# Layer 0 of a hybrid convolution and attention kernel: x's first products on whole columns, the group sums later, and the copies of the last inverse placed around the exponential

## The chip, the cores and the metric

The kernel runs on one core of one Trainium2 chip. The metric is the device time of one execution in microseconds (us). Three executions of the kernel before gave 2968.66, 2972.97 and 2974.31 us, so the median is 2972.97 us. A profile was taken of a further execution, which took 2970.21 us.

## The reference, cut to what matters

The program is two layers on x of shape (4, 32, 128, 128): 4 batches, each of 32 images of 128 x 128 float32. Layer 0 is a neural operator with attention, layer 1 is an additive attention with a mixture of experts. Only layer 0 is touched here. Of it this matters:

```
x = x + L0(_gn(x))                      # _gn: 32 groups along the last axis
...
xn = _inorm(xa)                         # each image for itself
k = _fno_layer(xn, Kcw, Ksw, 64, 64)    # 32 heads: low modes times weights, and a skip
q = _fno_layer(xn, Qcw, Qsw, 64, 64)
v = _fno_layer(xn, Vcw, Vsw, 128, 128)
scores = einsum('bntk,bnsk->bnts', q, k) / 64
p_attn = softmax(scores)                # 32 x 32 for each head
av = einsum('bnts,bnsk->bntk', p_attn, v)
p = _fno_layer(av, Pcw, Psw, 128, 128)
a = _inorm(p + xa)
m = _fno_layer(_inorm(a), m0cw, m0sw, 128, 128, inner_norm=True, act=True)   # gelu
m = _fno_layer(m, m1cw, m1sw, 128, 128, inner_norm=True)
out = _inorm(m) + a
```

An `_fno_layer` is a real Fourier transform of an image, a product with complex weights on the low modes, and the inverse transform. All transforms are done here as matrix products with tables of cosines and sines.

## The kernel before, in words

Layer 0 is `layer0` (L131). It handles the four batches one after the other (the loop `for b in range(B)`, L895); layer 1 follows, from about 890 us on, with an order of its own that is written out by hand and isn't touched.

**Who sets the order.** In layer 0 a planner orders the instructions of each engine. It goes by program order as a priority, by its own estimate of the durations, and by buffers. Tiles come from pools; tiles of one tag share a ring of so many buffers (`bufs`), and a tile waits for its ring's next buffer. The helper `behind(later, earlier)` (L144) adds an order between two instructions without any data between them. PSUM has the tags "a", "b" and "wide", each a ring of two. SBUF has among others the tags "z" (2), "v" (3), "pr" (6) and "fold" (2).

**Opening.** x of batch 0 is loaded, `image_rows` and `image_moments` (L386, L410) sum each image and its square, `group_moments` and `image_scales` (L422, L438) turn that into the factor and offset of each group. `image_scales` also spreads factor and offset of the 32 groups over all partitions: the product `bg` with a matrix of ones, tag "a" (L448), copied to `by_group`, which is read only in the value stage (L925). `value_weights` (L600) and L813 to L834 prepare the weights of values, keys and queries on VectorE.

**Spectra of x**, `spectra_of_images` (L481), in four groups of 8 images. `half_rows` (L285) multiplies each image as the stationary operand with 66 of the 128 columns of the table `rows`: the products `pz`, tag "a", four images to a tile, which ScalarE copies to `z`. `columns_of` (L495) multiplies two images of `z` with 68 of the 101 columns of `colg`: the products `it`, tag "b", copied to `fold`. `unfold` (L509, products `em` and `std`) makes the modes `xe`, `xm` and `xx` of 16 images; `edge_row` (L562) makes a single further mode. `image_weights` (L465) makes the factor of each image from the sums `my`, tag "a", placed behind the first group.

**Attention weights**, `attention_weights` (L645). `xp` is a copy of `xe` in PSUM, `hm` a masked copy of `xx`. The products `so` (L669) and `sp` (L700, from products `pa` on VectorE and `pb` on GpSimd or VectorE) give the scores `sc` (L715 to L725), with `spt`, a copy of `sp`, in between (L705). VectorE takes maximum and difference, ScalarE the exponential `ex` (L732), VectorE sum and reciprocal, GpSimd the product `ph` (L742). `ph` goes to DRAM and comes back as `pr` (L758, L762).

**Value stage** (L945 to L998). For 5 slices of modes and 4 groups of images, `xb` is broadcast from DRAM, copied to PSUM as `xw`, multiplied with the table `gb` of value weights (products `u`: L972 on GpSimd, L976 on VectorE, tag "pr"), and summed on TensorE with `pr` as `po` (L909). Products of `turn` and `skip` (`pxt`, `sk`) come in between. The table `gb` is made once, in the opening, by `spread_values` (L623): 32 products `gw` in two passes each, tag "wide", each pair copied by ScalarE. `skip_matrix` (L767) makes `bd` from `ph` with the products `cm`, the VectorE products `cd` (tag "v") and the sums `cp`.

**Rest of a batch.** Inverse transform, spectra of layer m0 (L1156), gelu, then the spectra of layer m1 (L1248), with the products `pz` of `first_step` (L305, 128 columns, tag "a"). The last inverse brings m1's modes `spec` back: `negative` (L1066) puts a negated copy in front of the modes, `row_products` (L334) gives `y` for 16 images in two tiles of the tag "wide", ScalarE copies four images at a time to `v`, `inv` turns these to `four` (L359, tag "b"), and VectorE adds `four` to the batch's `xr`, each image with its own factor `c3` (L1344). ScalarE scales the gelu's images, `g` = `c2` x `g` + `cq`, in 32 instructions (L1296), GpSimd adds them to `xr` in four (L1306).

**Passage from one batch to the next.** While the m1 part of batch b is under way, the next batch's `image_scales` (L1246), `spectra_of_images` (L1288) and `attention_weights` (L1333) run too. Three hooks put batch b's scaling in between: 16 scalings behind `hm` and ahead of `spt`, 8 behind `spt` and ahead of the exponential, 8 behind the exponential. The last inverse of batch b follows (L1361). All products of the value stage of batch b + 1 are ordered behind the last `four` of that inverse (`mixed = [inverted]`, L905).

Of the kernel before, what the change touches and what calls it, by code (L numbers as in the profile page):

```python
# [13 lines left out]
P = 128  # L14
# [116 lines left out]
def layer0(  # L131
# [153 lines left out]
    def half_rows(images, z, last):  # L285

        for k in range(0, GI, 4):
            pz = ps.tile([P, 4, 2, KY], F32, name="pz", tag="a")
            for j in range(4):
                mm = nc.tensor.matmul(  # L290
                    pz[:, j],
                    images[k + j],
                    rows.rearrange("p (r x) -> p r x", r=2)[:, :, :KY],
                    start=True,
                    stop=True,
                )
# [37 lines left out]
    def row_products(spec, a, ahead=()):  # L334


        wide = [ps.tile([P, 2, 512], F32, name="y1", tag="wide") for _ in range(2)]
        for slot in range(4):
# [22 lines left out]
    def back(spec, a, take, ahead=(), copy=None, apart=False):  # L361

        wide = row_products(spec, a, ahead)
        for g in range(4):
            four, inverted, _ = four_images(
                wide,
                g,
                copy or evacuate,
                dict(tag="pr", bufs=6) if apart and a else dict(tag="v", bufs=3),
                "a" if apart and g % 2 else "b",  # L370
            )
            take([image(a, g, k) for k in range(4)], four)
# [65 lines left out]
    def image_scales(sv, gm, gv, shift):  # L438
# [5 lines left out]
        both = small.tile([P, 2, 32], F32, name="both", tag="both")  # L444
        nc.vector.tensor_scalar(both[:, 0], of_group, gr, None, ALU.mult)
        nc.vector.tensor_scalar(both[:, 1], of_group, gs, -1.0, ALU.mult, ALU.mult)
        by_group = small.tile([P, 2, 32], F32, name="by_group", tag="by_group")
        nc.vector.tensor_copy(by_group, sums("bg", ones, both, "a"))  # L448
# [14 lines left out]
        return by_group, colg, shift, sv, sv_op  # L463
# [17 lines left out]
    def spectra_of_images(b, xt, normed, then=None):  # L481


        _, colg, shift, sv, _ = normed
# [10 lines left out]
        def columns_of(g, z):  # L495
# [3 lines left out]
            it = ps.tile([P, GI // 2, 2 * n], F32, name="it", tag="b")  # L499
            for j in range(GI // 2):  # L500
                mm = nc.tensor.matmul(
                    it[:, j], z[:, 2 * j : 2 * j + 2].rearrange("p t r x -> p (t r x)"), colg[:, : 2 * n], start=True, stop=True
# [4 lines left out]
            nc.scalar.copy(folded[g // half][:, k : k + GI // 2], it)  # L507
# [74 lines left out]
        for g in GROUPS:  # L582
            z = grp.tile([P, GI, 2, 32], F32, name="z", tag="z")
            made = half_rows([xt[:, g + t] for t in range(GI)], z, z32[:, :, g : g + GI])
            if g == 0:
                ysc, scaled = image_weights(sv, made)
            if g == GI and then is not None:
# [10 lines left out]
        return xx, (xe, xm), xd, edges, ysc  # L598

    def value_weights():  # L600
# [8 lines left out]
        behind(nc.vector.tensor_scalar(p1, pw[:, :, :KA, 0], hv[:, 3:4], None, ALU.add), normed[4])  # L609
        of_row = []  # L610
        for ri, (b, d, op) in enumerate(
            ((v_re, v_im, ALU.subtract), (v_im, v_re, ALU.add))
        ):
            g = grp.tile([P, KX // 4, KY], F32, name=f"g{ri}", tag="v", bufs=3)
            behind(nc.vector.tensor_scalar(g, pw[:, :, :, ri], hv[:, 2:3], None, ALU.mult), normed[4])
# [7 lines left out]
    def spread_values(of_row):  # L623

        n = KX * KY // 8
        picked = grp.tile([P, 2, 4, 8, 16], F32, name="picked", tag="z")
        for k in range(2):
            nc.scalar.copy(picked[:, k], steps(ident[:, 64 * k :], [1, 4], [0, 8], [4, 16]))
        for q in range(4):
            for k in range(2):  # L630
                rows_of = picked[:, k, q].rearrange("p s n -> p (s n)")
                for ri in range(2):
                    to = ps.tile([P, 2, 512], F32, name="gw", tag="wide")[:, :, :n]
                    for h in range(2):
                        nc.tensor.matmul(
                            to[:, h], rows_of, of_row[ri][:, n * h : n * h + n], start=True, stop=True
                        )
                    nc.scalar.copy(
                        gb[:, k, ri, 2 * n * q : 2 * n * q + 2 * n].rearrange("p (h m) -> p h m", h=2), to
                    )  # L640
# [4 lines left out]
    def attention_weights(b, front, hooks=None):  # L645

        xx, (xe, xm), _, (x32, w32), _ = front
        xs = per_image("xs")
        nc.vector.tensor_copy(xs, xx[:, :, KY])
# [8 lines left out]
        nc.scalar.activation(hm[:, :, 1:], xx[:, :, 1:masked], AF.Identity, scale=high)  # L658
# [1350 lines left out]
```

## Time and profile before

| What | Value |
|---|---|
| Median of three executions | 2972.97 us |
| Profiled execution, whole | 2970.21 us |
| Profiled execution, span from first to last instruction | 2968.5 us |
| Busy: TensorE, VectorE, ScalarE, GpSimd | 2754.0, 2187.5, 2323.7, 2028.2 us |
| Granted TensorE clock, mean | 0.979 of full |
| Opening: first instruction to the first product `po` | 0 to 83.35 us |
| First passage: last gelu of batch 0 to the first `po` of batch 1 | 217 to 291 us |
| Time from one passage to the next | 205 us |

How to read it: "PE" is TensorE's products, "PEld" its weight loads, "DVE" VectorE, "ACT" ScalarE, "POOL" GpSimd, "SP" the queue that issues DMAs. L12 is line 12 of the kernel. A float32 product is two instructions in the trace. In a timeline a line gives start, duration, engine, line, operation, out<-in, shape and how many; in brackets is the idle time of the engine before it and what ended that. In the chain of waits a line gives start, duration and what.

### The profile page before, as it was taken

How to read it: one execution, taken by the hardware profiler on the slowest of the kernel's cores; microseconds unless marked ns; L12 is line 12 of the kernel's file. 1: busy time of each engine (PE TensorE's matmuls, PEld its weight loads, DVE VectorE, ACT ScalarE, POOL GpSimd, SP SyncE). 2: the span in 40 equal slices, each digit the busy share in tenths (PEclk: the TensorE clock that was granted, in tenths of full speed). 3: DMA queues.
4: the chain of work that ended last, by engine and by line, in shares of the span. 5: the costliest groups of instructions: out<-in, count | busy, mean ns of one | idle time of the engine just before them, and what ended most of it. 6: DMA issues, size and time to landing. Idle time of an engine off the chain costs nothing.

```text
span 2968.5 us, 52711 instructions
## 1 busy us (share of the span) xinstructions
PE 2754.0 (93%) x19506; PEld 1364.1 (46%) x19506; DVE 2187.5 (74%) x4934; ACT 2323.7 (78%) x3235; POOL 2028.2 (68%) x1801
## 2 busy tenths in 40 slices
PE   8888988988878999999899999989999999999997
PEld 5465564664644443344444343444444343444443
DVE  4876787778866677775678688667778766878877
ACT  3554555456359999899899999989999998999991
POOL 1703605417208987878987878898787889798773
PEclk8998999999989999999999999999999999999998
DMA  3403304205021101002010100111010020000000
GB/s 93 126 1 70 117 1 106 81 9 152 14 61 33 33 1 40 8 16 57 1 26 15 26 15 8 42 25 31 15 26 15 10 56 15 26 13 21 15 15 14
DMA packets 151154, 107.72 MB, mean 36 GB/s; under 512 B 36303, under 2 KB 140018, under 8 KB 150898
## 3 DMA queue, kind: packets, MB, share of 16 engines
q1 hardware_dynamic: 147633, 102.26, 13.3%
q8 instruction: 154, 2.52, 0.4%
q10 hardware_dynamic: 3264, 2.10, 0.3%
q14 instruction: 103, 0.84, 0.1%
HBM read 63.86 MB, written 19.50 MB: 28 GB/s over the span
## 4 chain that ended last, share of the span: by engine, by line
PE 60%; POOL 12%; ACT 11%; DVE 10%; issue 6%; DMA 0%; POOLq 0%; DVEq 0%; ACTq 0%
PE d L1799 20%; PE po L1818 11%; PE px L1705 6%; ACT r L1849 5%; PE n L1799 4%; POOL e L1858 3%; PE po L909 3%; POOL e L1857 3%; POOL u L972 2%; ACT e L1865 2%; DVE r L1854 2%; POOL kx L1464 2%; PE pz L305 2%; DVE xc L1709 1%; PE px L1106 1%
## 5 line engine op out<-in xcount | busy, mean ns | idle before, releaser
L1854 DVE TENSOR_TENSOR r<-n,r 128x1024 f32<-128x1024 f32 (+1 forms) x1056 | 961.5, 952 | 478.6 <-PE n L1799 391.1
L1857 POOL TENSOR_TENSOR e<-r 128x512 f32<-128x512 f32 x528 | 674.0, 1277 | 270.2 <-DVE r L1854 269.6
L1849 ACT ACTIVATE r<-d 128x1024 f32<-128x1024 f32 (+1 forms) x1056 | 793.4, 803 | 64.7 <-PE n L1799 56.8
L1861 ACT ACTIVATE r<-r 128x1536 f32<-128x1536 f32 x528 | 783.6, 1484 | 16.7
L1858 POOL TENSOR_TENSOR e<-e,r 128x512 f32<-128x512 f32 x528 | 671.6, 1272 | 41.4
L1799 PE MATMUL d<-qe,ke 32*128 32x512 f32 (+3 forms) x2304 | 606.4, 602 | 39.4 <-ACT r L1849 35.0
L1818 PE MATMUL po<-e,kx 128*128 128x512 f32 (+3 forms) x1152 | 594.8, 605 | 17.4 <-POOL e L1870 17.4
L1799 PE MATMUL n<-qe,ke 32*128 32x512 f32 (+3 forms) x2304 | 606.3, 602 | 0.0
L1799 PE MATMUL n<-qf,kf 32*128 32x512 f32 (+3 forms) x2304 | 553.1, 555 | 0.0
L1799 PE MATMUL d<-qf,kf 32*128 32x512 f32 (+3 forms) x2304 | 551.8, 555 | 0.0
L1709 DVE SCALAR_TENSOR_TENSOR xc<-px,wgt,xc 128x128 f32<-128x128 f32 x1024 | 358.0, 350 | 42.1 <-PE px L1705 10.6
L1865 ACT ACTIVATE e<-e 128x512 f32<-128x512 f32 x528 | 325.8, 617 | 66.6 <-POOL e L1858 65.7
L1818 PEld LDWEIGHTS po<-e,kx 128*128 128x128 f32 x1152 | 175.8, 188 | 395.2 <-issue 309.7
L1799 PEld LDWEIGHTS d<-qe,ke 32*128 32x128 f32 x2304 | 176.6, 183 | 358.8 <-ACT r L1849 339.1
L1799 PEld LDWEIGHTS d<-qf,kf 32*128 32x128 f32 x2304 | 220.5, 186 | 175.7 <-issue 163.4
L1705 PE MATMUL px<-we,x2t 128*128 128x512 f32 x512 | 265.7, 605 | 6.7 <-DVE xc L1709 5.5
L972 POOL TENSOR_TENSOR u<-xb,gb 128x858 f32<-128x858 f32 (+1 forms) x112 | 219.7, 1994 | 56.9 <-PE po L909 53.3
L1799 PEld LDWEIGHTS n<-qf,kf 32*128 32x128 f32 x2304 | 228.3, 185 | 19.5 <-issue 11.7
L1123 POOL TENSOR_TENSOR spec<-part,part 128x512 f32<-128x512 f32 x16 | 25.3, 1578 | 304.0 <-DVE part L1120 110.8
L976 DVE TENSOR_TENSOR u<-xw,gb 128x858 f32<-128x858 f32 (+1 forms) x208 | 214.8, 1101 | 5.1 <-PE po L909 2.9
L1799 PEld LDWEIGHTS n<-qe,ke 32*128 32x128 f32 x2304 | 177.6, 183 | 9.4 <-DVE r L1854 0.9
L909 PE MATMUL po<-u,pr 128*32 128x429 f32 (+1 forms) x1280 | 150.4, 525 | 27.3 <-POOL u L972 17.7
(421 smaller groups left out, 3398.5 us busy)
## 6 DMA issues: line engine op xcount, KB each, us to landing
xb<-xd SPq DMA_DIRECT2D x128, 214.5 KB
xc<-x SPq DMA_DIRECT2D x29, 512.0 KB
x<-x SPq DMA_DIRECT2D x16, 512.0 KB
qf<-qe SPq DMA_DIRECT2D x64, 128.0 KB
out<-xc SPq DMA_DIRECT2D x15, 512.0 KB
x<-in_x SPq DMA_DIRECT2D x14, 512.0 KB
xb<-xd SPq DMA_DIRECT2D x32, 198.0 KB
kf<-ke SPq DMA_DIRECT2D x32, 128.0 KB
```

What stands on the lines that cost most here:

```text
L909: mm = nc.tensor.matmul(*args, **kw)
L972: weighed = nc.gpsimd.tensor_tensor(u, xb, gk, ALU.mult)
L1705: nc.tensor.matmul(px, x2t[:, k * P : (k + 1) * P], we[:, e0 : e0 + 4], start=True, stop=True)
L1709: nc.vector.scalar_tensor_tensor(xc[:, k], px[:, e], wgt[:, k, e0 + e : e0 + e + 1], xc[:, k], ALU.mult, ALU.add)
L1799: nc.tensor.matmul(o, k, q, start=turn == 0 or g > 0, stop=turn == 1 or g > 0)
L1818: nc.tensor.matmul(sums[c, h][:, q0 : q0 + c1 - c0], kx[:, jb], e[:, c0:c1], start=jb == 0, stop=is_last and q0 > 2 * P, skip_group_check= ...
L1849: nc.scalar.activation(r[:, g], d, AF.Ln, scale=1.0 / DSCALE)
L1854: nc.vector.tensor_tensor(r[:, g], part, r[:, g], ALU.mult)
L1857: nc.gpsimd.tensor_tensor(e, r[:, 1], r[:, 2], ALU.add)
L1858: nc.gpsimd.tensor_tensor(e, e, r[:, 0], ALU.add)
L1861: nc.scalar.activation(r, r, AF.Exp, scale=-1.0)
L1865: nc.scalar.activation(e, e, AF.Exp)
```

## The change

All edits are in layer 0.

1. `half_rows` uses all 128 columns of `rows`, `columns_of` all 101 of `colg`; the copies that follow take the same part as before.
2. `bg` and `by_group` leave `image_scales`. The product stands behind the third group's `pz` in `spectra_of_images`, and ScalarE copies it. In the opening, `my` stands behind the second group, not the first.
3. Opening: key and query weights come ahead of `value_weights`. Three of the value weights' steps go from VectorE to ScalarE, behind the last copy of `fold`. All `gw` products are behind the last `sc`; 9 of the 16 copies stay on ScalarE, 7 go to VectorE, and all but the first two are behind the exponential or the reciprocal.
4. `xs` and `xh` are made by ScalarE.
5. Batches 0 to 2: GpSimd multiplies the modes `spec` by the factor (`c3s`, made of `c3` by two VectorE operations), behind the second row's products `pb`; VectorE adds `four` in one instruction of 512 elements. The adds of the first half are behind the reciprocal.
6. Batches 0 to 2: the scalings are placed 4 ahead of `hm`, 24 behind `xh` and ahead of `spt` (with `negative` after the 16th image), 4 behind `spt`. Half of the first `row_products` is behind the last product of `sp`, half behind the last of `sc`. The first copy `v` and its `four` stand ahead of the exponential, the others behind it. The copies `xw` are behind the last copy `v`.

```diff
-            pz = ps.tile([P, 4, 2, KY], F32, name="pz", tag="a")
+            pz = ps.tile([P, 4, 2, KX], F32, name="pz", tag="a")
...
-                    rows.rearrange("p (r x) -> p r x", r=2)[:, :, :KY],
+                    rows.rearrange("p (r x) -> p r x", r=2),
...
-    def row_products(spec, a, ahead=()):
-        wide = [ps.tile([P, 2, 512], F32, name="y1", tag="wide") for _ in range(2)]
-        for slot in range(4):
+    def row_products(spec, a, ahead=(), slots=range(4), wide=None):
+        wide = wide or [ps.tile([P, 2, 512], F32, name="y1", tag="wide") for _ in range(2)]
+        for slot in slots:
...
-    def back(spec, a, take, ahead=(), copy=None, apart=False):
-        wide = row_products(spec, a, ahead)
+    def back(spec, a, take, begun=(), copy=None, apart=False):
+        wide, *ready = begun or [row_products(spec, a)]
         for g in range(4):
-            four, inverted, _ = four_images(
...
+            four, inverted, roots["v"] = (
+                ready[g]
+                if g < len(ready)
+                else four_images(
...
-        both = small.tile([P, 2, 32], F32, name="both", tag="both")
-        nc.vector.tensor_scalar(both[:, 0], of_group, gr, None, ALU.mult)
-        nc.vector.tensor_scalar(both[:, 1], of_group, gs, -1.0, ALU.mult, ALU.mult)
-        by_group = small.tile([P, 2, 32], F32, name="by_group", tag="by_group")
-        nc.vector.tensor_copy(by_group, sums("bg", ones, both, "a"))
...
-                    it[:, j], z[:, 2 * j : 2 * j + 2].rearrange("p t r x -> p (t r x)"), colg[:, : 2 * n], start=True, stop=True
+                    it[:, j], z[:, 2 * j : 2 * j + 2].rearrange("p t r x -> p (t r x)"), colg, start=True, stop=True
...
-            if g == 0:
+            if g == (GI if b == 0 else 0):
                 ysc, scaled = image_weights(sv, made)
+            if g == 2 * GI:
+                groups = sums("bg", ones, both, "a")
+                behind(summing["bg"], made)
+                nc.scalar.copy(by_group, groups)
...
-        behind(nc.vector.tensor_scalar(p1, pw[:, :, :KA, 0], hv[:, 3:4], None, ALU.add), normed[4])
+        behind(nc.scalar.activation(p1, pw[:, :, :KA, 0], AF.Identity, bias=hv[:, 3:4]), roots["fold"])
...
-            g = grp.tile([P, KX // 4, KY], F32, name=f"g{ri}", tag="v", bufs=3)
-            behind(nc.vector.tensor_scalar(g, pw[:, :, :, ri], hv[:, 2:3], None, ALU.mult), normed[4])
+            g = grp.tile([P, KX // 4, KY], F32, name=f"g{ri}", tag="fold")
+            behind(nc.scalar.activation(g, pw[:, :, :, ri], AF.Identity, scale=hv[:, 2:3]), roots["fold"])
...
+                        behind(mm, scored)
...
+                    if ri and (q or k):
+                        behind(nc.vector.tensor_copy(part, to), inverted)
+                    else:
+                        copied = nc.scalar.copy(part, to)
+                        if q or k:
+                            behind(copied, softmax)
...
-        nc.scalar.activation(hm[:, :, 1:], xx[:, :, 1:masked], AF.Identity, scale=high)
-        copied = nc.scalar.activation(hm[:, :, 0], xx[:, :, 0], AF.Identity, scale=half_high)
+        ahead = hooks[4](copied) if hooks else None
+        copied = nc.scalar.activation(hm[:, :, 1:], xx[:, :, 1:masked], AF.Identity, scale=high)
+        if ahead is not None:
+            behind(copied, ahead)
+        nc.scalar.activation(hm[:, :, 0], xx[:, :, 0], AF.Identity, scale=half_high)
...
+        nc.scalar.copy(xs, xx[:, :, KY])
+        copied = nc.scalar.activation(xh, xx[:, :, KY], AF.Copy, scale=0.5)
...
+            if yy == 1 and hooks:
+                hooks[5](on_pool)
...
                     if x0 == 0:
-                        behind(c, weights[4])
+                        behind(c, roots["v"] if b else weights[4])
...
+            def first_ones(copied):
+                for t in range(ones_ahead):
+                    act = scale(t)
+                    behind(act, copied)
+                return act
+            def factored(on_pool):
+                product = nc.gpsimd.tensor_tensor(
+                    spec[:, :, 64:], spec[:, :, 64:], c3s.unsqueeze(2).to_broadcast([P, GI, P]), ALU.mult
+                )
+                behind(product, on_pool)
             def first_half(copied, on_pool):
-                for t in range(T // 2):
+                for t in range(ones_ahead, late_ones):
                     act = scale(t)
                     behind(act, copied)
+                    if t == 2 * GI - 1:
+                        behind(negative(spec, slice(0, GI)), act)
...
+            def third_quarter(scores, copied):
+                for t in range(late_ones, T):
+                    act = scale(t)
+                    behind(act, copied)
+                ready.append(act)
+                begun.append(row_products(spec, 0, (scores,), range(2)))
+                return add_scaled(images_of[2])
+            def begin(scored):
+                row_products(spec, 0, (scored,), range(2, 4), begun[0])
+                begun.append(four_images(begun[0], 0, nc.scalar.copy))
+                behind(begun[1][2], ready[0])
+                return begun[1][2]
...
-                for j, t in enumerate(images):
-                    nc.vector.scalar_tensor_tensor(
-                        xr[:, t], four[:, j], c3[:, t : t + 1], xr[:, t], ALU.mult, ALU.add
-                    )
+                g = images[0] - 16 * a
+                to = xr[:, 16 * a : 16 * a + 16].rearrange("p (k t) c -> p k t c", k=2)[:, :, g : g + 2]
+                added = nc.vector.tensor_tensor(to, to, four.rearrange("p (k t) c -> p k t c", k=2), ALU.add)
+                if a == 0:
+                    behind(added, weights[7])
```

## The prediction, made before the changed kernel was run

> **What bounds the kernel now.** I read the page's first part, then the busy times by stretch, then the chain of waits of the first 320 us, then each engine's timeline in the two places that the change touches. Tensor work fills 93% of the span, but layer 1 (from about 890 us) is not touched; only layer 0 can move, and there the chain runs through the opening (0 to 93 us) and, three times, through the passage from one batch to the next (217 to 292 us in the first). The stretches (us, then busy time with its count of TensorE, weight loads, VectorE, ScalarE, GpSimd, then granted clock, DMA share, GB/s):
>
> ```profile
> 22.00:46.00 24.00, 23.89 (x138) 22.53 (x138) 10.57 (x49) 8.18 (x28) 0.00 (x0) 0.51 0.00 1
> 221.00:225.00 4.00, 0.52 (x3) 0.43 (x3) 3.72 (x14) 0.01 (x1) 1.26 (x1) 0.76 0.00 0
> 225.00:235.00 10.00, 9.87 (x85) 7.55 (x84) 4.68 (x11) 1.98 (x4) 0.00 (x0) 0.76 0.01 2
> 278.00:293.00 15.00, 12.48 (x86) 5.06 (x84) 12.44 (x37) 4.08 (x8) 5.20 (x4) 0.90 0.39 105
> 293.00:355.00 62.00, 56.51 (x718) 30.55 (x720) 53.54 (x53) 37.32 (x83) 50.04 (x26) 1.00 0.52 158
> ```
>
> The opening's products of x run with TensorE full at half clock for 24 us. At 221 TensorE stands still. The value stage (293 to 355) is filled by three engines at once, so its length stays and its start decides.
>
> TensorE's timeline, opening and first passage:
>
> ```profile
> 18.77 0.38 PE L380 MATMUL mg<-tot,cst 128*128 128x2 f32 x2 [0.60 <-DVE tot L425]
> 21.79 0.66 PE L380 MATMUL bg<-both,ones 128*128 128x64 f32 x2 [2.64 <-DVE both L446]
> 220.70 0.38 PE L380 MATMUL d<-y,cst 128*128 128x32 f32 x2 [0.56 <-DVE y L1040]
> 224.57 0.69 PE L380 MATMUL bg<-both,ones 128*128 128x64 f32 x2 [3.48 <-DVE both L446]
> 225.05 3.73 PE L305 MATMUL pz<-cst,g 128*128 128x128 f32 x16
> ```
>
> In both, pz comes right behind bg, though its operands were there: x had landed by 12.9 (its last square starts then), g's gelu ended at 217.2. It is the order that waits: bg and pz share the PSUM ring "a" of two.
>
> From the chain of waits (start, us, what):
>
> ```profile
> 30.08 5.12 PE pz L290 x24
> 169.54 1.79 PE pz L305 x16
> 225.26 3.52 PE pz L305 x16
> 239.22 3.57 PE pz L290 x32
> ```
>
> One pz instruction of 66 columns takes 5.12/24 = 213 ns at half clock and 3.57/32 = 112 ns at full; one of 128 columns 3.52/16 = 220 and 1.79/16 = 112. So width is free.
>
> The last inverse, on TensorE, ScalarE, VectorE and GpSimd:
>
> ```profile
> 271.45 3.17 ACT L1296 ACTIVATE g<-g,cq,c 128x128 f32<-128x128 f32 x8
> 274.53 1.52 ACT L357 COPY v<-y 128x512 f32<-128x512 f32 x3
> 275.14 3.78 PE L359 MATMUL four<-v,cst 128*128 128x512 f32 x4 [4.37 <-ACT v L357]
> 285.62 1.27 ACT L357 COPY v<-y 128x512 f32<-128x512 f32 x2 [7.78 <-PE y L343]
> 288.93 2.13 PE L359 MATMUL four<-v,cst 128*128 128x512 f32 x4 [0.69 <-ACT v L357]
> 290.06 2.16 DVE L1344 SCALAR_TENSOR_TENSOR x<-four,c,x 128x128 f32<-128x128 f32 x8 [0.25 <-PE four L359]
> 292.06 2.00 POOL L972 TENSOR_TENSOR u<-xb,gb 128x858 f32<-128x858 f32 x1 [9.80 <-PE po L909]
> ```
>
> Eight scalings stand between the exponential and the first copy of v; TensorE idles 4.37 us; po is tied behind the last four, and GpSimd waits 9.80 us for it.
>
> [...] 24 us of 66- and 68-column products did not release it. [...] Here a one-column VectorE product beside a GpSimd add took 1.16 us (222.87), else 0.16.
>
> **The change, part by part.**
>
> *Opening, order.* Without bg in front, pz can start when its bank is released (18.5) and mg is out (19.1), not at 22.45: -3.3. `my`, also on ring "a", comes only behind the second group, about when its input is ready (23.8 before).
>
> *Opening, clock.* pz goes from 66 to 128 columns, it from 68 to 101, at no cost (above). With pz from 19.1 there is no idle window before 22, and 128-column products let the clock go after at most two windows in the passage (half from 223 to 229.9 there). The stretch from 22.45 to the last std at 49.37 is 26.9 us. At full clock: pz 64 x 0.112 = 7.2, it 4 x 0.9 = 3.6, em and std (2 x 0.8 + 2 x 1.25) = 4.1, my, bg and edge 1.3: 16.2. Of the 10.7 I take 8, since ScalarE's copies and one cold window can come between (0 to 10.7). Key weights (8 VectorE operations of 0.45, some small) now fit in VectorE's 7.0 us hole before 43.26.
>
> *Opening, values.* 16 of the 64 gw products no longer sit among sp: from the first pa to the last sc took 20.0 us (49.71 to 69.72), in the passage 16.05 (252.95 to 269.0): -4. Against it stand the 8 VectorE operations of 0.43 of the value weights, which now fall here: +1.5. After sc all 64 gw stand: 64 x 0.237 (36 in 8.54) = 15.2, then cm 1.1 and 0.8 to po: 17.1 against 13.6 now: +3.5. The probabilities (GpSimd product, two DMAs) need about 13, so gw is last. VectorE takes 7 of 16 copies; TensorE at 0.95 a pair is slower than either copier at 0.6. Together: -3.3 - 8 - 4 + 1.5 + 3.5 = about **-10.5**.
>
> *Passage, group sums.* pz starts at 221.1 (after d) or before, not at 225.05: -4.0. Without that idle window the clock stays up: 16 pz and the first px cost 3.52 + 1.07 now, 2.2 less at full. bg, its ScalarE copy (about 0.2) and a bank wait come back in the third group: +0.4. `my` needs sv, at 226.8 now, earlier than TensorE reaches it. Sum -5.8, three times **-17.4** (0 to -8 each: pz may even slip in front of the stats).
>
> *Passage, around the exponential.* ScalarE: 4 scalings (0.386 each) take the gap 252.92 to 254.34; then hm, the two copies xs and xh (bound 0.15 to 0.25 each by 0.17 on VectorE and 0.36 for hm's column; I take 0.2), 24 scalings 9.3 and the negation 0.63 (its row now). That ends at 266.0; sp is ready at 266.3, where ScalarE had waited 4.78 us. So no cost, but the cover is 0.3 us. Then spt 1.0, four scalings 1.55, one v copy 0.57, the exponential some 0.2 later. Half of y (32 x 0.034 = 1.1) fills TensorE's wait for spt, the other half follows sc: 270.1. First four at 270.7, not 275.14; remaining v copies at 271.7 to 273.2 with no scalings before them. VectorE: one add of 512 (0.70, as in L1025) for four of 0.26: 8 x 0.37 = 3 less; they wait for the reciprocal (272.7), two banks of four wait with them. Second half: y from 273.3, its v copies share a ring of three with cd, so the last follows cd's reductions: GpSimd's ph ends 275.9 (as now), cm 1.1, two cd 1.3, two cp 1.9. I get the last v at about 280.5 and the last four at 282, against 291.06: -9.0. pr's read (issued at 279.3 now) lands about then; xw's copies follow v's last. Added: GpSimd's product with c3s (1024 elements, 2.35 as the x add), inside its hole of 4.39 before 258.95; of_slot and its reduction on VectorE, 0.4. Three times **-27**.
>
> Last batch: unchanged. Stores of x1 stay behind pr's read on SP. Sum -10.5 - 17.4 - 27 = -55. The profiled execution took 2970.2 (span 2968.5 and 1.7 around it): 2915. The median of the runs lies 2.8 above it: **2917 to 2918**; I say 2917. Own range 2900 to 2928.
>
> **Rivals.**
> - *The second half stays behind ph and cd* (ring of three): v starts only after both cp, at 280.2, and four v at 1.2 end at 285; 3 us less each: 2926. For it: 285.62 and 287.28, where v waited (the second for cp). Against: y was done only at 285.5.
> - *Half clock stays in the opening*: [...] 101 columns are too few. -10.5 becomes -2.5: 2926.
> - *pz isn't freed*: the planner puts my or another user of ring "a" ahead. Passage -1 each, opening -7: 2935. For it: the order is a plan, not seen here.
> - *Slower: scalings ahead of hm.* The first four need cq, ready at 251.68, 0.72 us before xp. [...] hm, xs and xh queue behind them, and so, sp, spt and the softmax behind those. cq hangs on a chain of 9 us from ms (242.6). If cq comes d late, each passage loses d; from d = 18.3 (55/3) all is lost. That is the case if the planner, with the front earlier, puts the chain's small VectorE operations behind the sp stage's 10.1 us of VectorE work: cq 10.1 + 9 + 1 after xp, d = 20.5, 2973 + 3 x 20.5 - 55 = 2979. Against: the chain stands ahead of that work in the program, and its last energies move up with px.
>
> **Chances.** Forecast 0.56, ring 0.14, clock 0.08, pz not freed 0.14, slower 0.05, within 0.2% 0.03. The range, 2898 to 2938, takes in the first four with a little on either side for the unknown copies; what is left out is the last two and the tails. 0.2% (6 us) is about what a measurement of this kernel can tell from no change. Faster 0.92, same 0.03, slower 0.05.
>
> **What would show it.** Opening: pz before 20 us, clock near 1.0 from 22 to 40, first po near 73 (83.35 now). Passage: no idle before bg, no half clock there; one four before the exponential; last four some 13 us after sc's end (22 now); GpSimd's wait of 9.8 shrunk below 2. Wrong would be: ScalarE's scalings ending after sp, or po waiting for pr instead of four.

## The result and the profile after

The changed kernel took 2922.35 us (median of four executions, 2921.58 to 2926.90) against 2973.64 us for the kernel before (four, 2968.66 to 2974.48). The ratio is 0.983, with a 95% interval of 0.982 to 0.985: 51 us faster, where 55 were forecast. The profiled execution, the slowest of the four (2926.9 us, span 2925.1), lies 43.3 us under the profiled one of before. By the last gelu of layer 0 it is 46.4 us ahead. Of these, 3.0 us are lost again in layer 1, which isn't touched: its first stage has 10 us more of half clock in this profile (37.5 us of it between 785 and 866, 27.3 in the same stage before). So the traces show 46.4 us in layer 0; what the medians differ by beyond that lies between executions, and these two traces don't show it.

Both traces, cut at the same events (us; "passages" gives one value for each of the three):

| Stretch | before | after | predicted change |
|---|---|---|---|
| start to the first `pa` | 49.71 | 37.23 | -9.8 |
| opening, first `pa` to last `sc` | 20.01 | 16.47 | -4 |
| opening, last `sc` to first `po` | 13.63 | 18.58 | +3.5 |
| passages, last gelu to first `pa` | 35.8, 37.6, 35.9 | 29.4, 29.4, 30.0 | -5.8 |
| passages, first `pa` to last `sc` | 16.1, 15.3, 16.3 | 16.5, 16.5, 16.5 | 0 |
| passages, last `sc` to first `po` | 22.0, 22.0, 20.8 | 16.3, 16.1, 16.1 | -9 |
| first `po` to last gelu, batches 1 to 4 | 133.8, 129.9, 129.5, 133.0 | 133.3, 129.3, 128.9, 134.3 | 0 |

The +1.5 for the value weights is counted in the first row, since six of their eight VectorE products and sums run ahead of the first `pa` in the kernel after.

These are the busy times by stretch of the kernel after, with columns as in the prediction (the granted clock is the third number from the end):

```profile
18.00:23.00 5.00, 4.92 (x29) 4.92 (x30) 3.56 (x26) 1.74 (x9) 0.00 (x0) 0.66 0.08 29
23.00:37.00 14.00, 13.35 (x163) 11.80 (x161) 10.41 (x49) 7.21 (x28) 0.00 (x0) 1.00 0.17 22
205.50:235.00 29.50, 27.73 (x326) 23.26 (x325) 23.93 (x100) 13.80 (x47) 3.38 (x3) 1.00 0.06 9
251.50:267.70 16.20, 12.48 (x116) 6.55 (x116) 12.51 (x18) 6.88 (x13) 11.71 (x7) 1.00 0.47 123
```

The opening's x steps run at full clock from 23 us on, with a single stretch of 3.4 us at half ahead of that (0.66 in the first row); before, the clock was 0.51 for 24 us. The passage from gelu to `pa` (205.5 to 235) has no half clock and TensorE is busy for 27.7 of 29.5 us.

TensorE's timeline in the kernel after, at the end of the opening and in the first passage:

```profile
53.63 3.00 PE L638 MATMUL gw<-g,picked 128*128 128x264 f32 x12
56.91 12.91 PE L638 MATMUL gw<-g,picked 128*128 128x264 f32 x52 [0.28 <-ACT gb L646]
72.28 0.93 PE L926 MATMUL po<-u,pr 128*32 128x429 f32 x8 [1.40 <-issue]
...
215.01 0.49 PE L290 MATMUL pz<-cst,x 128*128 128x128 f32 x2
223.71 0.41 PE L383 MATMUL bg<-both,ones 128*128 128x64 f32 x2
```

pz of the next x is now woven into layer m1's products from 215.0 on, and `bg` comes without an idle stretch before it (3.48 us before). In the opening the 64 `gw` take 16.2 us in a row.

For the last inverse, these are lines from the timelines of TensorE, VectorE, GpSimd and ScalarE of the kernel after:

```profile
236.81 1.90 POOL L1350 TENSOR_TENSOR spec<-spec,c3s 128x1024 f32<-128x1024 f32 x1
236.86 1.88 DVE L556 COPY xx<-par 1x16 f32<-1x16 f32 x1
...
258.98 2.12 PE L342 MATMUL y<-cst,spec 32*128 32x128 f32 x52
260.76 3.96 POOL L989 TENSOR_TENSOR u<-xb,gb 128x858 f32<-128x858 f32 x2
262.71 2.07 DVE L795 TENSOR_TENSOR cp<-cp,cst 128x32 f32<-128x32 f32 x1
262.76 1.07 ACT L356 COPY v<-y 128x512 f32<-128x512 f32 x2 [0.49 <-DVE cp L792]
265.02 1.28 DVE L1399 TENSOR_TENSOR x<-x,four 128x512 f32<-128x512 f32 x2
265.85 1.96 PE L358 MATMUL four<-v,cst 128*128 128x512 f32 x4 [2.03 <-DVE x L1399]
267.73 1.51 PE L926 MATMUL po<-u,pr 128*32 128x429 f32 x6
268.80 2.01 POOL L989 TENSOR_TENSOR u<-xb,gb 128x858 f32<-128x858 f32 x1 [4.08 <-PE po L926]
```

Read it from the end. `po` follows the last `four`. These products waited 2.03 us for a bank of PSUM that VectorE's add was to free. The add came late because a sum of 32 columns (L795) ahead of it took 2.07 us (0.19 before), and the sum took so long because GpSimd was at its `u` from 260.76 to 264.72. GpSimd itself had no use for the haste: it then waits 4.08 us for `po`. The first two lines are the same thing earlier on: a copy of 16 elements lasts as long as GpSimd's new product with `c3s`. Before, GpSimd was idle at both places (from 254.56 and from 282.25 on), and the copy and the sum were short:

```profile
254.86 0.16 DVE L554 COPY xx<-par 1x16 f32<-1x16 f32 x1
...
287.23 0.19 DVE L782 TENSOR_TENSOR cp<-cp,cst 128x32 f32<-128x32 f32 x1
```

### The profile page after: what moved, and what is told of

Same layout as the page of the kernel before. It is cut to its first block, busy times and chain, and to the rows that moved or that the text cites. A ratio compares the mean times of both kernels' runs of the same rounds, so it can differ in the third digit from the quotient of the medians.

```text
span 2925.1 us, 52645 instructions
## 1 busy us (share of the span) xinstructions
PE 2735.4 (94%) x19506; PEld 1352.7 (46%) x19506; DVE 2189.4 (75%) x4860; ACT 2322.9 (79%) x3243; POOL 2034.0 (70%) x1804
## 4 chain that ended last, share of the span: by engine, by line
PE 47%; POOL 11%; ACT 9%; issue 5%; DVE 5%; DMA 0%; POOLq 0%; SPq 0%; DVEq 0%; ACTq 0%
PE d L1854 20%; PE po L1873 12%; PE px L1760 6%; ACT r L1904 5%; PE n L1854 4%; POOL e L1913 3%; POOL e L1912 3%; ACT e L1920 2%; POOL kx L1519 1%; DVE r L1909 1%; DVE xc L1764 1%; POOL x L1519 1%; PE pl L1738 1%; POOL u L989 1%; ACT r L1916 1%
## 5 line engine op out<-in xcount | busy, mean ns | idle before, releaser
L1854 PE MATMUL d<-qe,ke 32*128 32x512 f32 (+3 forms) x2304 | 607.5, 603 | 39.9 <-ACT r L1904 35.8
L1920 ACT ACTIVATE e<-e 128x512 f32<-128x512 f32 x528 | 325.8, 617 | 66.0 <-POOL e L1913 65.1
```

The lines of the kernel that those rows point to most:

```text
L1854: nc.tensor.matmul(o, k, q, start=turn == 0 or g > 0, stop=turn == 1 or g > 0)
L1920: nc.scalar.activation(e, e, AF.Exp)
```

## The experiments

All medians stand beside the kernel before on the same chip (2971.97 to 2972.77); "after" is 2922.35 us.

### Which part of the first 30 us of a passage does it: the width or the order

**narrow:** the changed kernel with the old widths.

```diff
-            pz = ps.tile([P, 4, 2, KX], F32, name="pz", tag="a")
+            pz = ps.tile([P, 4, 2, KY], F32, name="pz", tag="a")
...
-            it = ps.tile([P, GI // 2, NX], F32, name="it", tag="b")
+            it = ps.tile([P, GI // 2, 2 * n], F32, name="it", tag="b")
```

> The changed kernel with pz's products back at 66 columns and it's at 68; all else stays. My theory (the prediction's clock step): [...] the granted clock stays half from about 22 to the end of x's steps; first value product (po) at about 80 instead of 72.3, +8 us, 2930. In the passages the stretch of x's steps falls to half clock too if the theory is general: it would add up to 3 us each, 2939. Rival: the clock is released because TensorE no longer stands still before pz; width is nothing: first po within 1 us of 72.3, no half clock in the passages, 2922.

Measured: 2953.51 us (2951.9 to 2957.3), ratio 0.994 (0.993 to 0.996). First `po` at 81.1 instead of 72.3, so the +8 of the opening came (8.8). But each passage lost far more than the theory gave it: gelu to `pa` 37.1, 36.9, 37.0. The stretches of its trace:

```profile
21.00:47.00 26.00, 25.92 (x166) 22.71 (x166) 13.70 (x67) 7.59 (x29) 0.77 (x1) 0.50 0.08 12
214.00:232.00 18.00, 16.97 (x184) 13.70 (x174) 15.34 (x49) 8.61 (x24) 3.01 (x2) 1.00 0.00 1
232.00:246.00 14.00, 13.56 (x87) 12.20 (x87) 4.44 (x28) 4.10 (x20) 0.00 (x0) 0.52 0.01 2
```

TensorE is busy for 16.97 of 18 us up to 232, with no idle stretch above 0.6 us, and still the clock falls to half at 232.4, some 7 us after the last product of more than 68 columns; it stays there for 13.65 us. So here the narrow products don't only fail to release the clock: it is lost while they run.

Their width alone doesn't explain that, though. In the kernel before, a stretch of 11.7 us without any product of more than 72 columns (234.8 to 246.4) ran at full clock and kept it. The same holds for the other two passages of that kernel and for all three of narrow_sums_early (below), with 11.5 to 12.4 us each. What differs is how often TensorE paused. The last 3.4 us ahead of the loss in narrow, then the narrow stretch of the kernel before:

```profile
229.00:232.40 3.40, 2.34 (x20) 2.06 (x19) 2.58 (x7) 1.54 (x6) 0.42 (x1) 1.00 0.00 0
```

```profile
236.00:246.00 10.00, 9.69 (x93) 9.48 (x95) 7.74 (x32) 6.14 (x27) 1.27 (x1) 1.00 0.00 0
```

In narrow TensorE waited twice for 0.53 us in these 3.4 us, for ScalarE's copies of `z`. Ahead of the losses in the other two passages it was busy for 2.79 and 2.56 of 3.4 us, and in the stretches that kept the clock for 2.87 to 3.40 of 3.4. So narrow products with more pauses between them lost the clock, and narrow products closer behind each other kept it. This is read from the traces, where the two lie close together; no run takes away the pauses alone.

**sums_early:** the changed kernel with `bg` back in `image_scales`, ahead of x's steps.

```diff
+        both = small.tile([P, 2, 32], F32, name="both", tag="both")
...
+        nc.vector.tensor_copy(by_group, sums("bg", ones, both, "a"))
         colg = small.tile([P, NX], F32, name="colg", tag="colg")
...
-            if g == 2 * GI:
-                groups = sums("bg", ones, both, "a")
```

> The changed kernel with the group sums (bg) back in front of x's steps, as before. My theory (the prediction's order steps): pz is tied behind bg again; opening +3.3, each passage +5.8 by the prediction, or +6.8 by the mean of what the traces show from the last gelu to the first pa (6.4, 8.2, 5.9): 2943 to 2946. Rival: x's steps start early because of the other moves (copies of xs and xh to ScalarE, my later), and bg costs only its own products: +1 to +2 each, 2926.

Measured: 2945.46 us (2940.2 to 2946.3). Gelu to `pa` 35.0, 35.8, 37.2 (+5.6, +6.4, +7.2), first `po` at 76.8 (+4.5). The order theory holds, its rival (+1 to +2) doesn't. In the first passage TensorE stands still for 3.49 us ahead of `bg` again, and the clock is at half from 215.1 to 221.9.

**narrow_sums_early:** both of the edits above together.

> The changed kernel with both taken back: 66 and 68 columns, and the group sums in front. Alone the narrow columns cost 7.1, 7.0 and 6.6 from a passage's gelu to pa and the early sums 5.6, 6.4 and 7.2, out of 6.4, 8.2 and 5.9 that the change gained there. My theory: each alone is enough to lose the clock, so together they cost hardly more than one: gelu to pa 36 to 38 (before: 35.8, 37.6, 35.9); in the opening they add up (8.8 and 4.5): first po at 84 to 86; 2956. Rival: the two are separate costs that add: gelu to pa 42 to 44, 2974.

Measured: 2958.87 us (2957.5 to 2960.5). This is within 3 us of the forecast 2956. The four kernels together, with the opening up to the first `pa` and then the three passages from gelu to `pa` (us):

| | early sums | late sums |
|---|---|---|
| 66 and 68 columns | 50.7; 37.1, 38.3, 37.6 | 46.5; 37.1, 36.9, 37.0 |
| 128 and 101 columns | 41.8; 35.0, 35.8, 37.2 | 37.2; 29.4, 29.4, 30.0 |

In the opening the two parts add: width 9.0 or 9.2, order 4.3 or 4.5. (Single profiles tell this to about 1 us: in the seven further runs below with this opening unchanged up to `pa`, the first `pa` came between 36.0 and 38.0.) In a passage they don't add. Width alone gives 0.4 to 2.5, order alone 0 to 1.4, both 7.6 to 8.9. There the clock is full on entry, and the traces show two ways in which it was lost. With early sums it falls at the standstill ahead of `bg` (3.49 us in sums_early, half from 215.1 to 221.9), is full again during layer m1's `pz` and `px` of 128 and 256 columns, and then stays up for narrow products too (the 11.5 to 12.4 us above). With late sums there is no standstill, and it falls in the stream of narrow products with pauses (narrow, at 232.4). Changing only one part leaves one of the two. Both products were always changed in width together, so that their shares aren't known.

**cols_96 and cols_80:** the changed kernel with 96 and with 80 columns in both products.

```diff
-                    pz[:, j],
+                    pz[:, j, :, : 48],
...
-                    rows.rearrange("p (r x) -> p r x", r=2),
+                    rows.rearrange("p (r x) -> p r x", r=2)[:, :, : 48],
```

> The changed kernel with 96 columns in the products of pz (128 in the changed kernel, 66 before) and in those of it (101, 68). One instruction takes 0.112 us at full clock at 66 and at 128 columns, so the array's columns are used about three quarters of the time here, and half of it at 66. Theory (a share between half and whole decides, 96 is above it): no half clock beyond single windows, first po 72 to 73, gelu to pa 29.4 in each passage, 2922. Rival (only full columns keep the clock): as with 66 columns, first po 81, gelu to pa 37, 2953.

> As the kernel with 96 columns, with 80 in both products (five eighths of 128). Theory: if the share that decides lies near one half, 80 is above it too: 2922. Rival: it lies between 80 and 96: first po about 81, gelu to pa 37, 2953. A time between the two would say that the share falls on both sides of it in different stretches.

Measured: 2927.52 us (2922.3 to 2930.1) and 2928.34 us (2925.6 to 2934.3), medians 5 and 6 us above the changed kernel, with a wide scatter. The profiled opening with 96 columns, then with 80:

```profile
23.00:37.00 14.00, 13.04 (x151) 10.94 (x150) 11.12 (x52) 6.73 (x24) 0.19 (x1) 1.00 0.15 22
```

```profile
23.00:37.00 14.00, 14.00 (x88) 13.45 (x87) 6.72 (x39) 3.82 (x17) 0.00 (x0) 0.50 0.01 2
```

With 96 columns everything is near the changed kernel (first `po` 71.6, gelu to `pa` 30.2, 30.6, 30.3). With 80 the profiled execution has both outcomes: in the opening the clock, lost at 19.4, stays at half for 30.7 us (first `po` 82.2), while in the passages it is hardly lost (30.2, 30.2, 31.0). That profiled execution is the slowest of its four. So 66 columns were too few in the opening, and in the passages of narrow; 80 were enough in the passages and not in the profiled opening; 96 was enough in the one profile. One profile for each can't place the edge closer. The share of the array's columns in use, by which the theory goes, is an estimate from the 112 ns of one instruction at 66 and at 128 columns; the runs show how the clock went with the width, not why.

### The last inverse: how much it gave, and where the rest stayed

**old_inverse:** the changed kernel with the scalings, copies, factor and adds of the last inverse as before.

```diff
-                added = nc.vector.tensor_tensor(to, to, four.rearrange("p (k t) c -> p k t c", k=2), ALU.add)
+                for j, t in enumerate(images):
+                    nc.vector.scalar_tensor_tensor(
+                        xr[:, t], four[:, j], c3[:, t : t + 1], xr[:, t], ALU.mult, ALU.add
+                    )
```

> The changed kernel with the last inverse as before: scalings of the last eight images around the exponential, no copies of v ahead of it, the factor c3 in VectorE's adds of 128 columns, no product with c3s on GpSimd. My theory: what the traces show from the last sc to the first po (16.2 after, 22.0, 22.0, 20.8 before) comes back whole, +5.4 each, less the 0.6 by which the stretch from pa to sc grew: +14 to +17, 2936 to 2939. Rival (the prediction's size): 9 each, 2949. Second rival: the gain between sc and po came from elsewhere (clock at full from 274 to 281): under +6, 2928.

Measured: 2935.76 us (2934.4 to 2939.9), +13, just under the forecast. `sc` to `po` 21.6, 20.9, 22.0 (+5.3, +4.8, +5.9), `pa` to `sc` 15.3, 15.2, 15.3 (-1.2 each). My theory's size holds but for the second term: what the new inverse costs ahead of `sc` is 1.2 a passage and not 0.6. From gelu to `po` a passage of the changed kernel is 4.0 us shorter than this one's on the mean (3.5 to 4.4), where the prediction had 9.

**cd_ring:** `cd` in the ring of z, so that the copies of v don't wait for `cp`.

```diff
-            cd = grp.tile([P, T, 16], F32, name="cd", tag="v", bufs=3)
+            cd = grp.tile([P, T, 16], F32, name="cd", tag="z")
```

> The changed kernel with cd in another buffer ring (z's) than v's, so that the third and fourth copy of v don't wait for cp's reductions. My theory: they then start 0.5 us earlier each, but the last products still wait for VectorE's adds: 0 to -0.3 each passage, 2921.5 to 2922.5. Rival of the prediction (the second half stays behind ph and cd): the ring is what keeps the last products 3 us late: -3 each, 2913.

Measured: 2922.44 us (2922.0 to 2924.0), `sc` to `po` 16.1 three times. The copies did move up, and nothing else did: the ring isn't what is late. (In this trace the small sum escapes with 0.19 us, and the next operation, `bd`, takes 2.01 instead, from 261.67 on, while GpSimd's `u` run from 259.57 to 263.53.)

**bd_late:** the sum and `bd` behind the last adds.

```diff
-        nc.vector.tensor_add(cp, cp, same)
+        return cp
+
+    def blocks(cp, after=None):
+
+        summed = nc.vector.tensor_add(cp, cp, same)
+        if after is not None:
+            behind(summed, after)
...
+            if a and b + 1 < B:
+                bd = blocks(cp, roots["last"])
```

> The changed kernel with the sum cp+same and the block bd behind the four adds of the last inverse's second half on VectorE, not between cp's reductions and those adds. My theory: in the first passage the sum of 32 columns took 2.07 us (0.19 before) because GpSimd's u (260.76 to 264.72) held VectorE's operands back; the adds behind it came at 265.02 instead of 262.9, the last products of four waited 2.03 for their bank, and po with them. So po comes 2 us earlier in each passage: -6, 2916. Rival (ring of three): the copies of v behind cd and cp set the end, the adds don't: under -0.5 each, 2921 to 2922.

Measured: 2921.36 us (2921.0 to 2924.8): no gain that can be told. Yet `sc` to `po` fell as expected, to 14.3 three times (-1.75 to -1.95). The time was lost again further on: from the first `po` to the last gelu batches 2 and 3 took 131.0 and 130.7 (129.3 and 128.9 in the changed kernel). VectorE's timeline of this kernel shows where:

```profile
267.46 1.71 DVE L799 TENSOR_TENSOR cp<-cp,cst 128x32 f32<-128x32 f32 x1
269.09 1.04 DVE L999 TENSOR_TENSOR u<-xw,gb 128x858 f32<-128x858 f32 x1
```

The sum meets GpSimd's next `u` (267.12 to 269.12) and again lasts until its end, 1.71 us, now in the value stage, which VectorE fills (15 `u` in 15.44 us from 270.25 on).

**combo:** bd_late, cd_ring, cm_early (below), and GpSimd's product with `c3s` ahead of its first `pb`.

```diff
-            if yy == 1 and hooks:
-                hooks[5](on_pool)
...
-                behind(product, on_pool)
```

> bd_late, cd_ring and cm_early together, and GpSimd's product with c3s ahead of its first pb (it stood idle 13.76 us before them) instead of behind them. My theory: with cd in another ring and the sum after the adds, the last products follow the copies of v: -2.5 to -3 from sc to po in each passage; without GpSimd's 1.9 us beside it, VectorE's 16-element copy to xx goes back from 1.88 to 0.16 and pa to sc goes from 16.47 to 15.3 as in old_inverse (15.25), -1.2 each; -2 in the first value stage: -13, 2909. Rival: pa to sc is bound by the pa products themselves or by sp, so nothing from c3s; -9, 2913. Second rival: something else behind (pr's transfer, the copies xw) holds po: -4, 2918.

Measured: 2926.32 us (2924.9 to 2928.8), slower than the changed kernel by 4; the forecast of 2909 was far off. `pa` to `sc` came down to 15.7, 15.4, 15.3, but gelu to `pa` rose to 31.5, 31.2, 31.9. VectorE and GpSimd of this kernel:

```profile
231.94 1.88 DVE L1303 TENSOR_SCALAR cq<-cq,par 128x32 f32<-128x32 f32 x1
...
231.89 1.90 POOL L1352 TENSOR_TENSOR spec<-spec,c3s 128x1024 f32<-128x1024 f32 x1 [10.39 <-DVE c3s L1322]
```

The product moved, and with it the collision: another small operation of VectorE is held for its 1.9 us, on a longer chain. TensorE then waits 2.38 us for an operation queued behind it on VectorE (`x`, L571), and the clock is at half from 234.0 to 240.9; how much of the 1.8 to 2.1 us from gelu to `pa` is the clock's wasn't separated. From the first `po` to the last gelu batches 1 to 3 took 132.4, 131.9 and 132.0 (130.9 in cm_early for the first, 131.0 and 130.7 in bd_late for the others): 0.9 to 1.5 us each are neither's alone, and stay open.

### The opening

**gw_ahead:** the first two `gw` tiles allowed among `sp`.

```diff
-                        behind(mm, scored)
+                        if q or k:
+                            behind(mm, scored)
```

> The changed kernel with the first two of the sixteen gw tiles allowed among the sp products of the opening (14 tiles still stand behind the last score). My theory: TensorE is two thirds idle among sp, and gw fills it from 53.6 to 69.8 afterwards, so two tiles at 0.98 us come off: first po 1.5 to 2 us earlier, 2920.5. Rival: products among sp hold the scores back as they did before (20.0 from pa to sc with 16 products among them against 16.5 now): sc later by 1.5, first po as now or later, 2922 to 2924.

Measured: 2925.85 us (2923.5 to 2926.1). The rival holds: `pa` to `sc` 19.2 instead of 16.5, first `po` at 75.8 instead of 72.3. A stretch at half clock from 37.8 to 41.2 isn't the reason: cm_early (below) has one from 38.4 to 41.8 and took 16.3 from `pa` to `sc`, and cols_96 has one from 38.6 to 42.1 and took 16.05. Behind `sc` it took 20.5 instead of 18.6, with the clock at half from 61.7 to 65.1. Part of the loss comes back later: from the first `po` to the last gelu batch 1 took 130.9 instead of 133.3.

**cm_early:** `skip_matrix` called ahead of `spread_values`.

```diff
+    bd = skip_matrix(weights[2], front[4])
     spread_values(picked, weights[5], weights[4], weights[7])
-    bd = skip_matrix(weights[2], front[4])
```

> The changed kernel with the opening's cm (and cd, cp, bd behind it) called before gw, so that TensorE does cm when ph is ready (61) and not after the last gw (70). My theory: TensorE's total before po stays, so po comes within 0.7 us of 72.3; but VectorE, which now does 3.2 of cd and cp between its first u (70.5 to 74.5) and lets TensorE wait 2.4 for u behind the first po, is done with them in its gaps of 1.25 among the copies of gb: -2 between the first po and the last gelu of batch 1, 2920. Rival: the value stage of batch 1 is set by its copies and by the DMA, and the wait moves on: 0, 2922.

Measured: 2920.94 us (2919.2 to 2924.6). `po` at 72.1, first `po` to last gelu of batch 1 130.9 instead of 133.3: the 2.3 us are there in the trace, in the medians no more than a hint.

### The collisions taken away

**best:** sum and `bd` go to GpSimd, ahead of its `u`; the 16-element copy goes to ScalarE; `cm` early as in cm_early.

```diff
-        nc.vector.tensor_add(cp, cp, same)
+        nc.gpsimd.tensor_tensor(cp, cp, same, ALU.add)
...
-        nc.vector.tensor_tensor(
+        roots["bd"] = nc.gpsimd.tensor_tensor(
             bd,
...
+                            if b:
+                                behind(weighed, roots["bd"])
...
-            nc.vector.tensor_copy(xx[:1, t, 0], bias)
+            (nc.scalar.copy if a else nc.vector.tensor_copy)(xx[:1, t, 0], bias)
```

> The changed kernel with three moves of small operations, all else kept: the sum cp+same and the block bd on GpSimd ahead of its first u (so they neither wait for GpSimd nor hold VectorE), the 16-element copy to xx of the second half of the images on ScalarE, and the opening's cm called before gw. My theory [...]: sc to po -1.75 in each passage as in bd_late, but without the +1.7 that bd_late gave back in the value stages of batches 2 and 3; pa to sc 16.47 to 15.3, -1.2 each; first value stage -2.3 as in cm_early: -11, 2911. Rival: GpSimd becomes what po waits for, since its u start 2 us later: sc to po as now, 2916. Second rival: pa to sc is set by GpSimd's pb, not by VectorE's copy: 2914.

Measured: 2912.81 us (five executions, 2910.6 to 2913.9), ratio 0.980 (0.978 to 0.981): 9.5 us under the changed kernel, and its slowest execution is under that one's fastest. GpSimd, VectorE and TensorE of this kernel in the first passage:

```profile
259.71 0.24 POOL L795 TENSOR_TENSOR cp<-cp,cst 128x32 f32<-128x32 f32 x1 [1.91 <-DVE cp L792]
260.39 7.96 POOL L989 TENSOR_TENSOR u<-xb,gb 128x858 f32<-128x858 f32 x4
...
260.08 1.48 DVE L1401 TENSOR_TENSOR x<-x,four 128x512 f32<-128x512 f32 x2 [0.44 <-PE four L358]
...
258.84 4.02 PE L358 MATMUL four<-v,cst 128*128 128x512 f32 x8 [0.73 <-ACT v L356]
262.80 1.87 PE L926 MATMUL po<-u,pr 128*32 128x429 f32 x8
```

All eight instructions of the second half's four products run in one piece, and GpSimd's `u` follow one another without the wait of 4.08. `sc` to `po` is 14.4 three times, `pa` to `sc` 15.3, and the value stages of batches 2 and 3 keep 129.3 and 129.0. In the passages all came as expected, and both rivals are out. The opening gave back 0.7 (`po` at 73.0): behind `sc` it took 20.9 instead of 18.6. TensorE waits 0.59 and 0.46 there for `ph` ahead of `cm`, and the clock is at half from 61.1 to 64.5; cm_early, which hasn't this stretch of half clock, took 19.6. The first value stage gained 2.5.

## Why the prediction was right, and where it was wrong

The time was right (2917, measured 2922), and so was the bulk of the mechanism; not all of the terms were. In the traces the gain in layer 0 is 46.4 us where 55 were forecast: the group sums gave 3 us more than their term, the last inverse 12 less. That the medians come within 5 us of the forecast is in part luck. Term by term:

- **Opening, -10.5 (the terms as written sum to -10.3): measured -11.1.** The order (-3.3) and the clock (-8) are confirmed apart from each other: 4.3 to 4.5 and 9.0 to 9.2 by the table of four, each about 1 us more than its term. With both taken back (narrow_sums_early) the first `pa` comes at 50.7, 1.0 behind the kernel before; the value weights had +1.5. The `gw` terms were +3.5 and -4 and came as +5.0 and -3.5. The 64 products took 0.253 each and not 0.237, and the wait ahead of `po` was 1.40 and not 0.8.
- **Passage, group sums, -5.8 each: measured -6.4, -8.2, -5.9.** The size is right and its reason only half. The prediction put all of it to the order (-4 for the standstill, -2.2 for the clock) and used the width in the opening alone. In fact the order gives little here without the width (0 to 1.4): with 66 columns the clock falls later instead. Undoing the width alone costs 31 us of the 51. What failed is the sentence that without the idle window the clock stays up: in narrow TensorE has no idle stretch above 0.6 us there, and the clock falls all the same (232.4).
- **Passage, last inverse, -9 each: measured -5.7, -5.9 and -4.7 behind `sc`, and +0.4, +1.2 and +0.1 ahead of it.** Three things were missed. Of the last `four` the prediction asked only when their v was there, not when their bank was free; behind the bank stood VectorE's queue, with the sum held by GpSimd: 1.7 to 1.95 us (bd_late, best). The product with `c3s` was said to fit GpSimd's hole at no cost; it fits, but holds VectorE's copy for its whole length: 1.2 us (best, old_inverse). The rest, about 1.5, is TensorE's order as the trace shows it, not tried: y of the second half was expected to end 6.5 us behind `sc` and ended 9.7 behind it (261.1 against 251.4), since two `four` and `cm` run between its fourth and its last products. Two of the signs that the prediction named didn't come: the last `four` end 16.4 us behind `sc` and not some 13, and GpSimd's wait is 4.08 us and not below 2.
- **The rivals.** "The second half stays behind ph and cd" gave 2926, nearer to the 2922 than the forecast, but for a wrong reason: cd_ring takes that wait away and gains nothing. Half clock in the opening and `pz` not freed didn't come. Scalings ahead of `hm` held nobody up: `hm` had its modes at 236.3 and ran at 236.41.

In the traces several small VectorE operations in SBUF lasted until the GpSimd instruction beside them was done. A sum of two tiles took 2.07 us (it ended at 264.78, GpSimd's `u` at 264.72) against 0.19 with GpSimd idle; the copy took 1.88 (238.74, `spec` 238.71) against 0.16; a tensor_scalar in combo took 1.88 (233.82, `spec` 233.79) against 0.24 for the same operation in the kernel after (231.33). Adds with an operand in PSUM took 0.69 beside GpSimd's `ph` (257.27 in the kernel after), as with GpSimd idle (266.98). Nor were the reductions `cp` held, although they too read and write SBUF: 1.02 and 1.04 beside GpSimd's add and `u` (259.98 and 261.63). The prediction had a case of such a wait (1.16 us), and then didn't ask of the operations that it moved whom they would meet.

## What to carry to other kernels

Ask of TensorE's clock not only whether the engine is busy, but how wide its products are and how closely they follow each other: one instruction took 112 ns at 66 columns and at 128, so the wider one was free here, and with it the clock held (1.00 from 23 to 37 us in the opening of the kernel after, 0.50 from 21 to 47 in narrow). A small VectorE sum or copy all in SBUF cost here as much as was left of the GpSimd instruction beside it, up to 2.07 us for the sum, which stood ahead of an add that frees a bank. Moving the sum later moved the collision (1.71 us in bd_late); giving the sum to GpSimd itself (0.24 us in best) and the copy to ScalarE (`pa` to `sc` 15.3 instead of 16.5) ended it. When two edits guard the same thing, undo each of them alone and both together before sharing out the gain: here undoing either one looks like the whole of it.

## What the runs showed of the hardware

- In the opening of narrow a stream of narrow products (66 to 72 columns for the most part), with TensorE busy for 25.92 of 26 us, ran at half clock throughout (0.50 from 21 to 47). In the first passage of narrow such a stream, with pauses of up to 0.53 us, lost the clock (1.00 from 214 to 232, half from 232.4). At 128 and 101 columns the opening ran at full clock with TensorE less busy, 13.35 of 14 us (1.00 from 23 to 37 in the kernel after). So the busy share in the profile didn't tell which clock was granted.
- In the traces of the kernels before and after every half-clock stretch lasted a multiple of 3.41 us, from 3.41 to 23.89, but for the last in each, which the span's end cuts off. The prediction's two windows from 223 to 229.9 are one such stretch, of 6.83 us.
- Keeping the clock and winning it back weren't the same: products of at most 72 columns kept it for 11.7 us in a passage of the kernel before (234.8 to 246.4), and failed for some 21 us to win it back in its opening (21.7 to 42.9). With 80 columns one and the same execution kept it in three passages (half in 0 to 3.4 us of each) and failed for 30.7 us in the opening.
- In the kernel after a GpSimd product of 128 x 1024 in SBUF took 1.90 us with the factor broadcast along the row (236.81); an add of that size with two full inputs took 2.35 (258.45).
